# Graph attention layer, one core: where the three products of a slot group are added up

## The chip, the cores and the metric

The kernel runs on one core of a Trainium2 chip. The metric is the time of one execution on the device in microseconds (us), the median of several runs. The engines of a core run side by side, each through its own queue, and meet at semaphores: TensorE (PE in the profile, its weight loads PEld), VectorE (DVE), ScalarE (ACT), GpSimd (POOL) and SyncE (SP). All matrices here are float32.

## The reference

One layer of attention over a graph with 4096 nodes of 512 features and 8 heads of 64, a feed-forward part, and a last normalization. The mask is sparse: a node has on average some 17 neighbours (itself among them), at most about 40.

```python
hs = layer_norm(x, ln1_scale, ln1_bias)          # sources
ht = layer_norm(h_target, ln1_scale, ln1_bias)   # targets
q = (ht @ Wq + bq).reshape(T, H, HD) / jnp.sqrt(jnp.float32(HD))
k = (hs @ Wk + bk).reshape(S, H, HD)
v = (hs @ Wv + bv).reshape(S, H, HD)
logits = jnp.einsum('thd,shd->hts', q, k)
logits = jnp.where(edge_mask[None] != 0, logits, NEG)
probs = jax.nn.softmax(logits, axis=-1)
ctx = jnp.einsum('hts,shd->thd', probs, v).reshape(T, D)
ht = layer_norm(ht + ctx @ Wo + bo, ln2_scale, ln2_bias)
x = _layernorm(x + ht + jax.nn.gelu(ht @ W1) @ W2)
```

## The kernel before

**Two stages.** The first (up to about 310 us) reads the adjacency matrix, makes for every node a list of its neighbours, sorts the nodes by their number of neighbours into 32 tiles of 128 rows, and projects all sources to k and v, which go to a table in DRAM (`kvd`, 1024 numbers a row: k, then v). The second does attention and feed-forward tile by tile. The tiles are in two parts of 16: tiles 0 to 15 hold the rows of the first half of the nodes, tiles 16 to 31 (`i >= NA`) those of the second. While the first part's attention runs, the lists of the second part are still being made; from tile 16 on there is attention and feed-forward only.

**Slot groups.** A tile whose rows have up to `cap` neighbours has `cap` slots: in slot j each of the 128 rows has its j-th neighbour. The slots are taken in groups of three (`S = 3`), with one or two left over at the end of a tile. There are 211 groups, 105 of them in tiles 16 to 31, and 95 of those have three slots. GpSimd gathers a slot's rows of `kvd` with an indirect DMA (line 966) into a ring buffer, `ring`, named `kv` in the profile: 20 slots in the second part, requested five groups ahead. For each group:

- VectorE multiplies q with k (line 1218) and sums it over each head's 64 elements to the logits `lg` (line 1223).
- ScalarE takes the exponential to `p` (lines 1227 and 1236).
- In a group of three, ScalarE also makes the product of the third slot (number 2) with its own exponentials: one small exponential (line 1199) and eight multiplications, one for each head (line 1202).
- VectorE multiplies the other slots' v with p in one instruction (line 1182).
- In tiles 16 to 31 VectorE adds the product of slot 1 to that of slot 0 (line 1186).
- TensorE transposes what is left, four blocks of 128 columns for each slot, and adds them up in PSUM as it does so (`cps`, line 1190). Tiles 0 to 15 send all three slots there, tiles 16 to 31 two: slots 0 and 2.

The products of a group are made by `values`, which runs one group later than its logits: the loop in `attention` issues the logits of group k, then the products of group k-1, then asks for new gathers (`request`). `by_scalar` is issued with the logits of its own group. A tile's last group is followed by `finish`: the sums of p (lines 1080 to 1087), the context times one over the sum (line 1101), the output projection (line 1113), and the second normalization (lines 697, 680, 692 and 1131, with a power on GpSimd in line 687). `front` makes q for a tile some groups ahead (lines 966, 1000, 1009, 1014).

**Feed-forward.** `feed` takes two tiles at a time: the hidden layer (line 1323), Gelu on ScalarE (line 1326), and the output (line 1332). `_weave` merges attention and feed-forward into one program by costs written in the code; these costs are not touched by the change. A scheduler of the language then sets the order of each engine's queue by its own estimates, so that an added instruction also moves others. Each queue runs in the order so set. After the last tile's attention TensorE still has feed-forward for about two tile groups to do.

Of the kernel before, what the change touches and what calls it, by code (L numbers as in the profile page):

```python
# [443 lines left out]
def adj_resnorm_kernel(  # L444
# [33 lines left out]
    nc = tc.nc  # L478
    N, D = x.shape
# [23 lines left out]
    S = 3  # L503
# [29 lines left out]
    with tc.tile_pool(name="keep", bufs=1) as keep:  # L533
# [17 lines left out]
        with ExitStack() as late:  # L551
# [481 lines left out]
            def step(gens, i):  # L1033

                if i in gens and next(gens[i], StopIteration) is StopIteration:
                    del gens[i]

            def request(k):


                ahead = AHEAD + (1 if k >= first_b else 0)
                while issued[0] <= min(k + ahead, len(SG) - 1):
                    issue(issued[0])
                    mine = set(range(place[issued[0]], place[issued[0]] + SG[issued[0]][2]))
                    for m in range(k, issued[0]):
                        assert not mine & set(range(place[m], place[m] + SG[m][2]))
                    issued[0] += 1
# [100 lines left out]
            def go_on():  # L1148
                for i in list(fronts):
                    step(fronts, i)  # L1150
# [14 lines left out]
            def attention():  # L1165


                tails, pend = [], []

                def advance():  # L1170
                    go_on()
                    for t in list(tails):
                        if next(t, StopIteration) is StopIteration:
                            tails.remove(t)

                def values(i, j0, n, kv, p, cps, after):

                    m = n - 1 if n == S else n  # L1180
                    v4 = kv[:, :m, D:].rearrange("p j (h d) -> p j h d", h=H)
                    nc.vector.tensor_tensor(v4, v4, p[:, j0:j0 + m, :].unsqueeze(3)  # L1182
                                            .to_broadcast([P, m, H, HD]), ALU.mult)
                    slots = list(range(n))
                    if m > 1 and i >= NA:
                        nc.vector.tensor_add(kv[:, 0, D:], kv[:, 0, D:], kv[:, 1, D:])
                        slots.remove(1)
                    for j in slots:
                        for c in range(KC):
                            nc.tensor.matmul(cps[:, c, :], kv[:, j, D + c * P:D + (c + 1) * P], ident,  # L1190
                                             is_transpose=True, start=j0 + j == 0 and c == 0,
                                             stop=j0 + n == TILES[i][1] and j == slots[-1],
                                             skip_group_check=True)
                    if after is not None:
                        tails.append(after)

                def by_scalar(kv, lg):
                    pa = sp.tile([P, H], F32, name="pa")
                    nc.scalar.activation(pa, lg[:, S - 1, :], AF.Exp)
                    for hd in range(H):  # L1200
                        v = kv[:, S - 1, D + hd * HD:D + (hd + 1) * HD]
                        newest[:] = [nc.scalar.mul(v, v, pa[:, hd:hd + 1]).ins]  # L1202

                request(0)
                yield 0.0
                k = 0
                for group in GROUPS:
                    hs = []
                    mv = sp.tile([P, 2, 2], F32, name="mv2")
                    cost = 0.5 * UNIT * len(group) / 2 / sum(TILES[i][1] for i in group)  # L1210
                    for i in group:
                        cps = ps.tile([P, KC, P], F32, name="cps", bufs=2)
                        while k < len(SG) and SG[k][0] == i:
                            _, j0, n = SG[k]
                            while i not in tqs:
                                step(fronts, i)
                            kv, tq = kvs.pop(k), tqs[i]
                            nc.vector.tensor_tensor(kv[:, :n, :D], kv[:, :n, :D],  # L1218
                                                    tq[:, :D].unsqueeze(1).to_broadcast([P, n, D]),
                                                    ALU.mult)  # L1220
                            lg = sp.tile([P, S, H], F32, name="lg")
                            latest[:] = [lg[:, 0, 0:1]]
                            nc.vector.tensor_reduce(lg[:, :n, :],  # L1223
                                                    kv[:, :n, :D].rearrange("p j (h d) -> p j h d", h=H),
                                                    AX.X, ALU.add)
                            if j0 > 0:
                                nc.scalar.activation(p[:, j0:j0 + n, :], lg[:, :n, :], AF.Exp)  # L1227
                            advance()
                            yield cost * n
                            if pend:  # L1230
                                values(*pend.pop())
                                request(k)
                            advance()
                            if j0 == 0:
                                p = sp.tile([P, MAXE, H], F32, name="p", bufs=1)
                                nc.scalar.activation(p[:, :n, :], lg[:, :n, :], AF.Exp)
                            if n == S:
                                by_scalar(kv, lg)
                            last = j0 + n == TILES[i][1]
                            after = finish(i, p, cps, group, hs, mv) if last else None  # L1240
                            pend.append((i, j0, n, kv, p, cps, after))
                            yield cost * n
                            k += 1
                values(*pend.pop())
                while tails:
                    advance()
                    yield 3.0
                verdict()

            def verdict():  # L1250

                sf = sums.rearrange("p t h -> p (t h)")
                both = sp.tile([P, MAXE, H], F32, name="p", bufs=1).rearrange("p j h -> p (j h)")
                ok, over = both[:, :NT * H], both[:, NT * H:NT * H + NT]
                nc.vector.tensor_scalar(ok, sf, SUM_LO, None, op0=ALU.is_gt)
                nc.vector.scalar_tensor_tensor(ok, sf, SUM_HI, ok, op0=ALU.is_lt, op1=ALU.mult)
                nc.vector.tensor_reduce(bad[:, 3:4], ok, AX.X, ALU.min)
                nc.vector.tensor_scalar(bad[:, 3:4], bad[:, 3:4], 1.0, None, op0=ALU.not_equal)
                for i, (_, cap) in enumerate(TILES):
                    nc.vector.tensor_scalar(over[:, i:i + 1], tags[:, i, DEG:DEG + 1], float(cap),  # L1260
                                            None, op0=ALU.is_gt)
                nc.vector.tensor_reduce(bad[:, 4:5], over, AX.X, ALU.max)
                nc.vector.tensor_scalar(over, tags[:, :, DEG], 1.0, None, op0=ALU.is_lt)
                nc.vector.tensor_reduce(bad[:, 5:6], over, AX.X, ALU.max)
                b1 = sp.tile([P, 1], BF16, name="b1", bufs=1)
                nc.vector.tensor_reduce(b1, bad, AX.X, ALU.max)
                pb = ps.tile([1, 1], F32, name="t", bufs=2)
                nc.tensor.matmul(pb, b1, ones_bf[:, 0:1], start=True, stop=True)
                nc.vector.tensor_scalar(raised, pb, 0.5, None, op0=ALU.is_gt)
# [215 lines left out]
```

## Time and profile before

| | us |
|---|---|
| median of 3 runs (lowest, highest) | 1821.51 (1818.98, 1823.71) |
| the profiled execution | 1820.38 |
| its span | 1818.6 |
| TensorE busy in the span | 1686.6 (93%) |
| VectorE busy | 1435.0 (79%) |
| ScalarE busy | 1221.5 (67%) |
| GpSimd busy | 976.5 (54%) |
| first, last addition of line 1186 (start) | 1028.0, 1682.8 |

The page cuts the span into 40 equal slices of 45.5 us and gives an engine's busy share of each in tenths (9 is 90% or more); PEclk is the clock that TensorE was granted. The groups of instructions give line, engine, operation, tiles and shape, then the count, and after the bar the busy time in us and the mean of one instruction in ns; after the second bar stands the time for which the engine idled before such an instruction, and what released it. A line of the waits gives who waited for whom, the total in us, the number of waits, and the longest. Busy times of neighbours can overlap, so the distance between two starts is what one more instruction costs a full queue.

### The profile page before, as it was taken

The numbers are of one execution on the slowest core, as the hardware profiler recorded it, in microseconds if no ns is written. First come the engines' busy times: TensorE is split into PE (matmuls) and PEld (weight loads), VectorE is DVE, ScalarE is ACT, GpSimd is POOL, SyncE is SP. The second block draws the span as 40 slices with busy tenths as digits, with TensorE's granted clock in tenths as the row PEclk, the third lists the DMA queues.
The fourth block names the chain that finished last, engine by engine and source line by source line (L and its number), as shares of the span: only waits on it lengthen the run. The fifth ranks groups of instructions, "written<-read, shape, count | busy, mean of one in ns | idle before, by whom it ended". The sixth has DMA issues, their size and how long they took to land. (4 is left out here: it accounts for less than half of the span.)

```text
span 1818.6 us, 22965 instructions
## 1 busy us (share of the span) xinstructions
PE 1686.6 (93%) x7030; PEld 1100.9 (61%) x7030; DVE 1435.0 (79%) x2660; ACT 1221.5 (67%) x3119; POOL 976.5 (54%) x834
## 2 busy tenths in 40 slices
PE   7999975588999999999999989999999999999997
PEld 3444432466766666676776657666666666666664
DVE  6989866899999837787978989979879697988200
ACT  5867644486998645767878878877877576787311
POOL 1000143666465576676668788877575655764101
PEclk9999987598999999999999999999999999999999
DMA  9999958989887747677879878887786767774000
GB/s 345 366 389 370 346 171 304 405 284 324 292 303 234 238 141 269 227 267 263 289 259 316 296 258 277 261 291 266 241 268 206 262 222 242 247 248 152 18 6 26
DMA packets 140268, 463.26 MB, mean 255 GB/s; under 512 B 16500, under 2 KB 21672, under 8 KB 140136
## 3 DMA queue, kind: packets, MB, share of 16 engines
q0 software_dynamic: 96656, 342.64, 55.7%
q1 hardware_dynamic: 35664, 95.98, 15.0%
q10 hardware_dynamic: 7816, 23.08, 3.3%
q8 instruction: 58, 0.95, 0.2%
q14 instruction: 74, 0.61, 0.1%
HBM read 430.75 MB, written 30.89 MB: 254 GB/s over the span
## 5 line engine op out<-in xcount | busy, mean ns | idle before, releaser
L966 POOL DMA_INDIRECT kv<-kvd,rec x603 | 757.4, 1256 | 370.7 <-PE cps L1190 134.1
L1332 PE MATMUL po<-w,gt 128*128 128x512 f32 x1024 | 466.3, 598 | 6.6 <-ACT gt L1326 6.3
L1323 PE MATMUL pf<-h2T,w 128*128 128x256 f32 (+1 forms) x2176 | 466.5, 368 | 2.0 <-issue 1.7
L1323 PEld LDWEIGHTS pf<-h2T,w 128*128 128x128 f32 x2176 | 389.5, 191 | 66.9 <-issue 22.1
L1202 ACT ACTIVATE kv<-kv,pa 128x64 f32<-128x64 f32 x1520 | 391.0, 336 | 4.4
L1218 DVE TENSOR_TENSOR kv<-kv,tq 128x1536 f32<-128x1536 f32 (+2 forms) x211 | 352.0, 1678 | 51.0 <-DMA kv<-kvd,rec 48.4
L1223 DVE TENSOR_REDUCE lg<-kv 128x24 f32<-128x1536 f32 (+2 forms) x211 | 350.6, 1669 | 1.0
L1332 PEld LDWEIGHTS po<-w,gt 128*128 128x128 f32 x1024 | 188.9, 192 | 203.2 <-issue 195.2
L1190 PE MATMUL cps<-ident,kv 128*128 128x128 f32 x2008 | 267.5, 281 | 45.3 <-issue 22.7
L1190 PEld LDWEIGHTS cps<-ident,kv 128*128 128x128 f32 x2008 | 240.9, 146 | 112.7 <-issue 69.8
L1182 DVE TENSOR_TENSOR kv<-kv,p 128x1024 f32<-128x1024 f32 (+1 forms) x211 | 251.4, 1196 | 26.3 <-ACT p L1227 21.1
L687 POOL TENSOR_TENSOR n_rs<-n_ve,mhalf 128x2 f32<-128x2 f32 (+2 forms) x51 | 50.1, 983 | 329.8 <-DVE n_ve L680 154.5
L728 ACT ACTIVATE kv<-kv 128x1024 uint8<-128x1024 int32 x128 | 134.9, 1055 | 97.4 <-DMA kv<-in_adj_dram 49.3
L1326 ACT ACTIVATE gt<-pf 128x512 f32<-128x512 f32 x128 | 76.4, 597 | 97.1 <-PE pf L1323 74.9
L929 PE MATMUL pq<-wk,h2T 128*128 128x512 f32 x256 | 125.3, 634 | 12.3 <-ACT h2T L914 5.5
L735 DVE MAX8 cand<-kv 128x8 uint16<-128x103 uint16 (+1 forms) x640 | 133.6, 259 | 0.5
L1326 ACT ACT_TABLE_LOAD x103 | 132.1, 1283 | 1.7
L1009 PE MATMUL t<-wq,tq 128*128 128x512 f32 x256 | 117.4, 602 | 5.0 <-ACT tq L1003 4.3
L929 PE MATMUL pq<-wv,h2T 128*128 128x512 f32 x256 | 115.3, 593 | 0.6 <-ACT tq L931 0.6
L1113 PE MATMUL t<-wo,rb 128*128 128x512 f32 x256 | 115.2, 592 | 0.0
L1227 ACT ACTIVATE p<-lg 128x24 f32<-128x24 f32 (+2 forms) x179 | 39.1, 219 | 105.7 <-DVE lg L1223 83.3
L929 PEld LDWEIGHTS pq<-wk,h2T 128*128 128x128 f32 x256 | 50.4, 204 | 78.1 <-issue 59.0
(159 smaller groups left out, 1582.2 us busy)
## 6 DMA issues: line engine op xcount, KB each, us to landing
kv<-in_adj_dram SPq DMA_DIRECT2D x128, 512.0 KB
kvd<-tq ACTq DMA_DIRECT2D x24, 512.0 KB
kv<-kvd,rec POOLq DMA_INDIRECT x603
kv<-in_L_gnn_h_target_dram SPq DMA_DIRECT2D x32, 256.0 KB
kv<-in_x_dram SPq DMA_DIRECT2D x15, 512.0 KB
rest_d<-gid SPq DMA_DIRECT2D x32, 160.0 KB
w<-in_L_gnn_W_dram SPq DMA_DIRECT2D x4, 1024.0 KB
kvd<-kv ACTq DMA_DIRECT2D x8, 512.0 KB
```

The lines of the kernel that those rows point to most:

```text
L728: nc.scalar.activation(sg, a, AF.Sign, accum_out=dpart[:, i, h:h + 1])
L735: nc.vector.max(cand[:, h * SQ + s, :], wd[:, w0:w1])
L929: nc.tensor.matmul(pkv, hT[:, kc, j * P:(j + 1) * P], w[:, kc, :], start=kc == 0, stop=kc == KC - 1)
L966: nc.gpsimd.indirect_dma_start(out=dst, out_offset=None, in_=table[:, :], in_offset=bass.IndirectOffsetOnAxis(ap=idx, axis=0))
L1182: nc.vector.tensor_tensor(v4, v4, p[:, j0:j0 + m, :].unsqueeze(3) .to_broadcast([P, m, H, HD]), ALU.mult)
L1190: nc.tensor.matmul(cps[:, c, :], kv[:, j, D + c * P:D + (c + 1) * P], ident, is_transpose=True, start=j0 + j == 0 and c == 0, stop=j0 + n ...
L1202: newest[:] = [nc.scalar.mul(v, v, pa[:, hd:hd + 1]).ins]
L1218: nc.vector.tensor_tensor(kv[:, :n, :D], kv[:, :n, :D], tq[:, :D].unsqueeze(1).to_broadcast([P, n, D]), ALU.mult)
L1223: nc.vector.tensor_reduce(lg[:, :n, :], kv[:, :n, :D].rearrange("p j (h d) -> p j h d", h=H), AX.X, ALU.add)
L1323: nc.tensor.matmul(pf[:, k, :], w1[(f0 + k) // KC][:, kc, (f0 + k) % KC * P:((f0 + k) % KC + 1) * P], h2T[:, kc, :w], start=kc == 0, stop= ...
L1326: nc.scalar.activation(gt, pf, AF.Gelu_apprx_tanh)
L1332: nc.tensor.matmul(po[j], gt[:, k, j * P:(j + 1) * P], w2[(f0 + k) // KC][:, (f0 + k) % KC, :], start=False, stop=f0 + k == FC - 1, skip_g ...
```

## The change

In a group of three slots in tiles 16 to 31, VectorE adds the product of slot 2 to slot 0 as well, with a second addition after the one of line 1186. TensorE then transposes slot 0 alone: four transposes instead of eight. Groups of one or two slots, and all groups of tiles 0 to 15, are as before. Lines after the addition move down by three; the second addition is line 1189 of the changed kernel.

```diff
                     if m > 1 and i >= NA:
                         nc.vector.tensor_add(kv[:, 0, D:], kv[:, 0, D:], kv[:, 1, D:])
                         slots.remove(1)
+                        if n == S:
+                            nc.vector.tensor_add(kv[:, 0, D:], kv[:, 0, D:], kv[:, S - 1, D:])
+                            slots.remove(S - 1)
                     for j in slots:
                         for c in range(KC):
                             nc.tensor.matmul(cps[:, c, :], kv[:, j, D + c * P:D + (c + 1) * P], ident,
```

## The prediction

> **What bounds the kernel now.** I read the page's slices first, then the second part cut into stretches, then its groups, then who waits for whom, then single instructions. All times are those of the one profiled execution: span 1818.6 us, 1820.38 us with what lies around it, 1.1 us under the median of three runs (1821.51 us).
>
> The slices, the page's second section:
>
> ```profile
> PE   7999975588999999999999989999999999999997
> DVE  6989866899999837787978989979879697988200
> PEclk9999987598999999999999999999999999999999
> ```
>
> The additions of line 1186 run only from 1028 to 1683 us, so only slices 23 to 37 can change. TensorE is full there, VectorE nearly; the last two and a half slices are TensorE alone. The same in numbers: busy time by stretch (columns: stretch, its length, then busy time and instructions of TensorE, of its weight loads, of VectorE, ScalarE and GpSimd, then granted clock, DMA share, GB/s):
>
> ```profile
> 1028.00:1178.00 150.00, 142.06 (x621) 96.67 (x620) 143.55 (x148) 122.39 (x335) 124.57 (x88) 0.98 0.83 274
> 1178.00:1328.00 150.00, 145.81 (x621) 97.68 (x620) 129.95 (x150) 115.15 (x306) 104.19 (x89) 0.99 0.77 254
> 1328.00:1478.00 150.00, 146.87 (x630) 99.70 (x629) 121.42 (x139) 105.66 (x281) 94.50 (x82) 0.99 0.75 250
> 1478.00:1628.00 150.00, 150.00 (x639) 100.92 (x638) 125.09 (x138) 109.06 (x293) 92.37 (x79) 1.00 0.72 239
> 1628.00:1700.00 72.00, 71.83 (x312) 48.82 (x311) 53.61 (x100) 48.21 (x124) 25.83 (x21) 1.00 0.40 132
> 1700.00:1818.60 118.60, 105.49 (x446) 70.27 (x444) 7.18 (x26) 20.73 (x40) 10.58 (x12) 0.96 0.06 19
> ```
>
> From 1028 to 1700 us TensorE is busy 656.6 of 672 us and VectorE 573.6. The reader is to see that the balance moves: in the first stretch VectorE is the fuller one (143.6 against 142.1), later TensorE. So TensorE bounds most of this part, VectorE its first fifth, and the margin between them is small everywhere.
>
> The groups the change touches, from 1028 to 1700 us:
>
> ```profile
> L1190 PE MATMUL cps<-ident,kv 128*128 128x128 f32 x789 | 104.4, 275 | 6.7 <-DVE kv L1186 6.6
> L1182 DVE TENSOR_TENSOR kv<-kv,p 128x1024 f32<-128x1024 f32 x100 | 121.6, 1220 | 14.1 <-ACT p L1227 14.1
> L1186 DVE TENSOR_TENSOR kv<-kv 128x512 f32<-128x512 f32 x101 | 68.8, 684 | 0.2
> ```
>
> **What the Trainium skill says.** "VectorE: DVE Perf Modes", section on the TRN2 errata, gives an fp32 tensor_tensor add as (N+151)/0.96 ns, 691 ns for 512 elements; the 684 ns above agree. "TensorE: Matmul & The Clock Gate", its table at the head, calls the queues of ScalarE and VectorE strict FIFOs: an instruction that waits holds all behind it. The order on both engines in the trace fits that. "SBUF — State Buffer", Who interferes with whom, says that a VectorE instruction with two SBUF inputs contends with a GpSimd instruction that reads SBUF; the new additions are of that kind. The gathers of line 966 take 933 ns at the least and 1285 ns in the mean here, but GpSimd is busy 441 of 672 us, so I give this no time.
>
> **The change part by part.** Tiles 16 to 31 have 95 groups of three slots. The order of the built program has 380 transposes fewer on TensorE and 95 additions more on VectorE, and nothing more or less on the other engines.
>
> TensorE, removed: single instructions (start, duration) give the price, since the 275 ns of one overlap the next.
>
> ```profile
> 1211.17 1.04 PE L1190 MATMUL cps<-ident,kv 128*128 128x128 f32 x8
> ...
> 1241.81 0.60 PE L1190 MATMUL cps<-ident,kv 128*128 128x128 f32 x4
> ```
>
> Four transposes more cost 1.04 - 0.60 = 0.44 us, so 95 groups save 41.8 us of TensorE's queue, not the 104 us that 380 times 275 ns would give. That comes to 6% of its work between 1028 and 1700 us. The tail is not touched: after the last transpose of line 1190 the built program has the same matmuls as before, and the tail's 118.6 us stay.
>
> VectorE, added: two neighbours of the same size start 0.60 us apart, though each lasts 0.68.
>
> ```profile
> 1139.44 0.68 DVE L1186 TENSOR_TENSOR kv<-kv 128x512 f32<-128x512 f32 x1
> 1140.04 0.68 DVE L1223 TENSOR_REDUCE lg<-kv 128x8 f32<-128x512 f32 x1
> ```
>
> I take 0.61 us, so 58 us for 95; VectorE goes from 573.6 to 631.6 us, TensorE from 656.6 to 614.8. The bound changes hands.
>
> The new wait: the second addition needs slot 2, which ScalarE multiplies head by head (line 1202, eight instructions); before, only TensorE read that row. Start, duration, engine:
>
> ```profile
> 1203.70 0.57 ACT L1202 ACTIVATE kv<-kv,pa 128x64 f32<-128x64 f32 x2
> 1204.29 1.28 ACT L1326 ACT_TABLE_LOAD   x1
> ...
> 1206.07 1.92 ACT L1144 ACTIVATE h2T<-t,cols 128x256 f32<-128x256 f32 x4
> ...
> 1206.39 0.68 DVE L1186 TENSOR_TENSOR kv<-kv 128x512 f32<-128x512 f32 x1
> ...
> 1207.87 1.55 ACT L1202 ACTIVATE kv<-kv,pa 128x64 f32<-128x64 f32 x6
> ```
>
> Here two products were done, then a table load, a Gelu and four copies came between, and the last product ended at 1209.42, 2.35 us after the first addition. Taken over the 95 groups, the products end after their first addition in 26, by 37.7 us together; by more than 1.7 us (one q times k product, which the new order usually puts between the two additions) in 8, by 10.4 us beyond it. So the wait costs between 0 and 38 us; I take 10 us for VectorE. Behind the waiting addition stand the next logits' reduction (line 1223) and the next product with p (line 1182); ScalarE's exponentials wait for the one, TensorE's transposes for both.
>
> The buffer's slot 2 now comes free with the second addition, slot 0 still with TensorE's transposes, which wait longer. The gathers are issued 11 us or more (19.5 in the median) before VectorE reads them, so a few microseconds are covered by that lead. If the cover went, the waits of line 1218 on its gathers, now 10.2 us, would grow; I count 0, at most 10.
>
> Order: the scheduler also pulls feed-forward matmuls forward. Before the transposes of slot group 123 (of 211) the program has some 28 more of them, counted in units of about 0.44 us (a pair of the 256-wide ones; sixteen last 3.62 us in the trace), and it is level again from group 179. That moves some 12 us of TensorE's work into the stretch where VectorE is the bound, and is worth about 4 us later.
>
> The sum, by stretch, with 24.5, 21.6, 19.8, 19.8 and 9.4 groups (the counts of line 1186, 26, 23, 21, 21 and 10, times 95/101): VectorE gets 158.5, 143.1, 133.5, 137.2, 59.3; TensorE 131.3, 136.3, 138.2, 141.3, 67.7. The larger ones make 648.8 us, if nothing idles. In the first stretch VectorE, the fuller engine, idled 4.3%. I charge that where VectorE leads or is within 5 us, 5% in the third, 2% in the last: 165.6 + 149.5 + 145.5 + 147.7 + 69 = 677.3, against 672: +5.3. Less 4 for the order, plus 10 for the wait, is +11: 1820.4 + 11 = 1831 us.
>
> **Rivals.**
> - TensorE stays the bound (faster). VectorE idled 98 us in these 672, and 30 of them were for a late TensorE: the waits on line 1009 and, through ScalarE, on line 1113.
>
> ```profile
> DVE kv L1182 <- ACT p L1227: 17.7, 11, 3.6
> DVE tq L1014 <- PE t L1009: 17.3, 5, 6.2
> DVE n_nm L692 <- POOL n_rs L687: 13.9, 7, 4.3
> DVE n_st L697 <- ACT h L1118: 12.6, 3, 6.1
> ```
>
> If the 58 us fit into that slack, the first stretch costs about 162 (2% idle), the others 146, 141, 141 and 68: 658, so -14, 1806 us. For it: 1278 to 1328 us, where VectorE was busy 47.6 of 50 us while TensorE never stopped. Against it: the remaining waits (ScalarE's p, GpSimd's powers) don't come from TensorE and stay.
> - Even: the idle share of the first stretch holds everywhere and the new wait falls into time VectorE would idle anyway: 1821 us.
> - The in-order wait spreads (slower, far). VectorE waits for products that stand on ScalarE behind a Gelu, which waits for TensorE, which waits in order for transposes behind the same addition. It decides from where the wait reaches its upper bound of 38 us and the old 68 us of other idle time stay: 631.6 + 38 + 68 = 738, +66; half of that wait and 50 us of the idle time give 701, +29: 1849 us.
> - That the change doesn't do what it says is excluded by the built order.
>
> **How the numbers follow.** VectorE as bound, +4 to +24 us: 0.45. Spread wait, +24 to +50: 0.15. Even: 0.18. TensorE's gain shows: 0.22, down to 1804. A measurement of this kernel tells 0.3%, 5.5 us, from no change. Part of the first case lies within it (0.03): slower 0.57, same 0.21, faster 0.22. Range 1804 to 1856; the likeliest case alone is 1824 to 1844.
>
> **What would show it.** Right: line 1190 has 1628 transposes, the new addition 95 times at 0.68 us; VectorE at 93% or more between 1028 us and the last addition; TensorE with waits of tens of microseconds on line 1189; waits of line 1189 on line 1202 near 10 us; the tail unchanged. Wrong: TensorE still at 98% there (then the time falls), or VectorE under 90% with long waits on line 1202 (then it rises more).

## The result, and the profile after

The changed kernel takes 1838.76 us (median of 11 runs, 1827.11 to 1843.23) against 1823.21 us before (11 runs, 1818.98 to 1830.21): ratio 1.0076, 95% interval 1.0054 to 1.0097 (the two medians alone give 1.0085). It is slower, by some 15.5 us where 9.5 were forecast. The two profiled executions lie a little further apart than the medians: the span is 1839.4 us, 20.8 more than before.

The slices of the changed kernel's page (as before, tenths of 40 equal slices):

```profile
PE   7999884598999998999999989979999899989997
DVE  6999867899998848777879989979989798988400
PEclk9999987698999999999999999989998999999998
```

Busy time by stretch of the changed kernel, with the columns of the prediction's table; the part that can change now ends at 1718 instead of 1700 us:

```profile
1028.00:1178.00 150.00, 137.51 (x550) 88.90 (x548) 141.69 (x161) 115.01 (x313) 110.99 (x82) 0.98 0.79 257
1178.00:1328.00 150.00, 135.43 (x520) 86.99 (x520) 135.73 (x158) 112.37 (x293) 118.18 (x85) 0.93 0.77 250
1328.00:1478.00 150.00, 132.92 (x516) 86.91 (x515) 131.33 (x155) 108.14 (x281) 113.73 (x83) 0.93 0.75 246
1478.00:1628.00 150.00, 142.76 (x559) 92.83 (x558) 140.30 (x174) 117.64 (x310) 106.77 (x75) 0.98 0.71 231
1628.00:1718.00 90.00, 82.98 (x315) 52.92 (x314) 77.62 (x125) 63.68 (x160) 40.91 (x33) 0.96 0.53 174
1718.00:1839.40 121.40, 108.36 (x457) 72.70 (x455) 7.90 (x30) 22.58 (x42) 11.30 (x13) 0.96 0.06 19
```

TensorE is no longer full, and VectorE is not full either: in every stretch both idle, by 7 to 19 us of 150, and almost equally. Two engines that idle together point to a common wait. From 1028 to 1718 us VectorE is busy 626.7 of 690 us, before 573.6 of 672: 53 us more work, 35 us less idle time, and the part is 18 us longer. The other 3 us of the span lie within the last row.

Where the idle time is, the waits of the changed kernel from 1028 to 1725 us say (who for whom: total us, times, longest):

```profile
ACT h L1131 <- DVE n_nm L692: 62.6, 8, 12.0
DVE n_nm L692 <- POOL n_rs L687: 53.5, 8, 10.2
...
PEld cps L1193 <- DVE kv L1189: 36.5, 24, 9.5
...
PE cps L1193 <- DVE kv L1189: 25.1, 7, 9.1
...
PE t L1140 <- ACT h L1131: 23.2, 7, 10.4
```

53.5 of VectorE's 63 us of idle time are one kind of wait: the mean of the second normalization (line 692) waits for GpSimd's power (line 687). Before, VectorE idled 21.7 us at line 692; the profile finds no releaser ("issue") for one of these waits, of 7.8 us:

```profile
L692 DVE SCALAR_TENSOR_TENSOR n_nm<-mv,n_rs 128x2 f32<-128x2 f32 x8 | 1.3, 160 | 21.7 <-POOL n_rs L687 13.9 <-issue 7.8
```

All its other waits together shrank from 77 to 10 us.

The second addition, in the groups of instructions over the same time, doesn't wait (0.1 us idle before it):

```profile
L1189 DVE TENSOR_TENSOR kv<-kv 128x512 f32<-128x512 f32 x95 | 65.0, 685 | 0.1
```

One of the eight waits in order of time, from the timeline of the changed kernel (start, duration, engine, instruction, and in brackets the idle time before it and its releaser):

```profile
1198.62 3.17 PE L1335 MATMUL po<-w,gt 128*128 128x512 f32 x7
...
1200.67 0.69 DVE L1186 TENSOR_TENSOR kv<-kv 128x512 f32<-128x512 f32 x1
...
1201.89 0.94 POOL L966 DMA_INDIRECT kv<-kvd,rec  x1 [0.30 <-PE po L1335]
1203.14 0.94 POOL L966 DMA_INDIRECT kv<-kvd,rec  x1 [0.31 <-issue]
1204.38 0.94 POOL L966 DMA_INDIRECT kv<-kvd,rec  x1 [0.30 <-issue]
1205.63 0.94 POOL L966 DMA_INDIRECT kv<-kvd,rec  x1 [0.30 <-issue]
1206.87 0.94 POOL L966 DMA_INDIRECT kv<-kvd,rec  x1 [0.30 <-issue]
1208.11 0.94 POOL L966 DMA_INDIRECT kv<-kvd,rec  x1 [0.30 <-issue]
1209.36 0.94 POOL L966 DMA_INDIRECT kv<-kvd,rec  x1 [0.30 <-issue]
1210.31 0.74 POOL L687 TENSOR_TENSOR n_rs<-n_ve,mhalf 128x2 f32<-128x2 f32 x1
1211.09 0.16 DVE L692 SCALAR_TENSOR_TENSOR n_nm<-mv,n_rs 128x2 f32<-128x2 f32 x1 [9.72 <-POOL n_rs L687]
...
1211.28 1.52 ACT L1131 ACTIVATE h<-h,n_nm,n_rs 128x512 f32<-128x512 f32 x2 [10.92 <-DVE n_nm L692]
...
1212.15 0.47 PE L1140 MATMUL t<-ident,h 128*128 128x128 f32 x1 [10.37 <-ACT h L1131]
```

The reader is to see that for some nine microseconds none of the compute engines works but GpSimd, which issues seven gathers, one every 1.24 us, before it comes to a power of two columns. The power's input had been ready since 1196.4. VectorE, ScalarE and TensorE each stand, in their own order, at the instruction that needs it.

In the built order the power's place is hardly new: before and after, it stands on GpSimd's queue behind the gathers that lie about five slot groups ahead of VectorE, and line 692 on VectorE zero to four instructions behind the variance. What is new is that GpSimd is behind when the power is asked for. Before, in four of the eight tile groups after 1028 us GpSimd began the power 0.15 us after its input was ready, with no DMA issued in between; now it does so in one, and in the other seven it first issues three to ten DMAs, and the power begins 3.7 to 13.9 us after its input. VectorE is in step with those places, where before it was often late for other reasons, TensorE among them. And GpSimd has become slower: a gather of line 966 takes 1395 ns in the mean where it took 1285.

### The profile page after: what moved, and what is told of

Same layout as the page of the kernel before. It is cut to its first block, busy times and chain, and to the rows that moved or that the text cites. A ratio compares the mean times of both kernels' runs of the same rounds, so it can differ in the third digit from the quotient of the medians.

```text
span 1839.4 us, 22352 instructions
## 1 busy us (share of the span) xinstructions
PE 1660.0 (90%) x6650; PEld 1062.8 (58%) x6650; DVE 1486.0 (81%) x2755; ACT 1237.1 (67%) x3129; POOL 1029.2 (56%) x834
## 5 line engine op out<-in xcount | busy, mean ns | idle before, releaser
L966 POOL DMA_INDIRECT kv<-kvd,rec x603 | 793.2, 1315 | 355.2 <-issue 119.9
L1335 PE MATMUL po<-w,gt 128*128 128x512 f32 x1024 | 479.9, 608 | 10.9 <-ACT gt L1329 10.9
L1326 PE MATMUL pf<-h2T,w 128*128 128x256 f32 (+1 forms) x2176 | 474.0, 370 | 0.3 <-ACT h2T L1144 0.3
L1193 PE MATMUL cps<-ident,kv 128*128 128x128 f32 x1628 | 225.9, 283 | 65.7 <-DVE kv L1182 40.3
L1193 PEld LDWEIGHTS cps<-ident,kv 128*128 128x128 f32 x1628 | 198.1, 146 | 134.6 <-DVE kv L1182 44.6
L687 POOL TENSOR_TENSOR n_rs<-n_ve,mhalf 128x2 f32<-128x2 f32 (+2 forms) x51 | 46.2, 905 | 319.2 <-DVE n_ve L680 151.1
```

The lines of the kernel that those rows point to most:

```text
L966: nc.gpsimd.indirect_dma_start(out=dst, out_offset=None, in_=table[:, :], in_offset=bass.IndirectOffsetOnAxis(ap=idx, axis=0))
L1326: nc.tensor.matmul(pf[:, k, :], w1[(f0 + k) // KC][:, kc, (f0 + k) % KC * P:((f0 + k) % KC + 1) * P], h2T[:, kc, :w], start=kc == 0, stop= ...
L1335: nc.tensor.matmul(po[j], gt[:, k, j * P:(j + 1) * P], w2[(f0 + k) // KC][:, (f0 + k) % KC, :], start=False, stop=f0 + k == FC - 1, skip_g ...
```

## The experiments

Three theories at the outset. *Queue*: the change loses because VectorE, now full, stands in order for a power that is stuck on GpSimd behind gathers. *Work*: VectorE's 58 us of additions set the time, and the standing only fills time that it would idle anyway. *Order*: any edit makes the scheduler lay the queues anew, and the luck of that order is what is measured. All ratios are to the kernel before, with 95% intervals.

**Line 692 later, in the changed kernel.**

```diff
                 rs = power(sp, mv[:, :nh, :], nh, "n2", ve)
                 yield
+                yield
+                yield
+                yield
+                yield
                 nm = negmean(sp, mv[:, :nh, :], rs, nh, "n2")
```

> The changed kernel, with the mean of the second normalization (line 692) and what follows it emitted four half-groups later after GpSimd's power (line 687); nothing else differs. Theory, queue: the changed kernel loses because VectorE, now full, stands at line 692 for a power that waits on GpSimd behind gathers (53.5 us in eight waits). Then these waits fall below 10 us, the last addition moves forward by 35 to 45 us, and the time is 1795 to 1810 us, ratio to before 0.985 to 0.993. Rival, work: VectorE's 58 us of additions set the time and the standing only fills time that it would idle anyway: 1830 to 1840 us, ratio 1.004 to 1.009.

Measured: 1802.23 us, ratio 0.9884 (0.9857 to 0.9910), within what *queue* gives. The waits of VectorE from 1028 to 1730 us:

```profile
DVE n_st L697 <- ACT h L1118: 18.7, 1, 18.7
DVE n_nm L692 <- POOL n_rs L687: 11.0, 3, 9.6
```

and the second stretch, busy time by engine as above:

```profile
1178.00:1328.00 150.00, 148.50 (x589) 93.47 (x588) 150.00 (x180) 126.36 (x327) 123.02 (x92) 1.00 0.80 275
```

The standing falls from 53.5 to 11 us, not quite below 10, and VectorE is busy for 150 of 150 us, TensorE for 148.5. *Work* is refuted: the same additions are done in less time than before the change. The last transposes of context end at 1673.3 us instead of 1722.3; the stretch after them has grown from 117.1 to 127.3 us. This version computes all that the reference asks for and beats both kernels. But its queues are laid anew in large part, so that this run alone doesn't part *queue* from *order*.

**The same half way: two half-groups later.**

> The changed kernel with line 692 and what follows emitted two half-groups later in place of four; seven to nine instructions of VectorE then stand between the variance and line 692, against two to four in the changed kernel and thirteen in the later version. Theory, queue: a dose in between: standing of 10 to 30 us, 1808 to 1825 us, ratio 0.991 to 1.000. Rival, order: the later version's 0.9884 was luck of the new order, and this one does not lie between them.

Measured: 1815.25 us, 0.9948 (0.9934 to 0.9963); VectorE stands 24.7 us at line 692. With 53.5, 24.7 and 11.0 us of standing the three versions take 1838.8, 1815.3 and 1802.2 us: a dose and its effect, into which luck of the order would hardly fall.

**The same edit in the kernel before.**

> The kernel before, with the same later place of line 692. Theory, queue: TensorE bounds this kernel, so the 21.7 us for which VectorE stands there between 1028 and 1700 us are worth little: 1810 to 1823 us, ratio 0.993 to 1.000. If later normalizations starve the feed-forward part: up to 1835 us. Rival, work: no change, 0.998 to 1.002.

Measured: 1853.65 us, 1.0162 (1.0135 to 1.0189); a miss. The edit didn't do here what it was for: the scheduler put line 692 directly behind the variance all the same in four of the first seven tile groups, and the standing grew to 35.2 us. The stretch after the last transposes grew by 10 us here as well (127.1 against 117.3 us). What else costs the time was not pursued. So an edit that lays the queues anew can cost over one per cent, and the later version's gain can't be taken to be the wait's alone; the next runs had to touch the wait with less disturbance.

**The product of line 692 on GpSimd**, in the changed kernel and in the kernel before:

```diff
+                ng = sp.tile([P, nh], F32, name="n2_ng")
+                nc.vector.tensor_scalar_mul(ng, mv[:, :nh, 0], -1.0)
                 yield
                 rs = power(sp, mv[:, :nh, :], nh, "n2", ve)
+                nm = sp.tile([P, nh], F32, name="n2_nm")
+                nc.gpsimd.tensor_tensor(nm, ng, rs, ALU.mult)
                 yield
-                nm = negmean(sp, mv[:, :nh, :], rs, nh, "n2")
```

> The changed kernel with the product of line 692 (minus mean times power) made by GpSimd right behind its power; VectorE makes only minus the mean, beforehand. VectorE no longer waits for GpSimd's power, but ScalarE still does at line 1131, in its own queue, and TensorE at line 1140. Theory, queue: the 53.5 us of standing at line 692 are gone; about half comes back as waits of VectorE for ScalarE's exponentials that stand behind line 1131: 1808 to 1825 us, ratio to before 0.991 to 1.001. If VectorE's own place in the queue was all: 1790 to 1805 us. Rival, work: no change against the changed kernel, 1834 to 1842 us.

> The kernel before with the same product on GpSimd. Theory, queue: with TensorE as bound the standing of VectorE is worth at most some us: 1812 to 1825 us, ratio 0.994 to 1.001. Rival, order: any such edit makes the scheduler lay the queues anew, and that alone moves the time by a per cent either way, as the later place of line 692 did in the kernel before (1.0162): then this lies outside 0.994 to 1.001.

Measured: changed 1865.24 us, 1.0216 (1.0196 to 1.0237); before 1832.04 us, 1.0037 (1.0020 to 1.0053). Both miss the expectation of *queue*; the second lies just outside its range, as *order* had it. The waits of the first show where the time went, ScalarE's and then VectorE's (in this version's numbers 1131 is the new product on GpSimd, 1134 the scaling on ScalarE that was line 1131, 1208 ScalarE's product of slot 2, 1192 the second addition, 1185 the product with p, 1242 the exponential of a tile's first group):

```profile
ACT h L1134 <- POOL n_nm L1131: 88.0, 7, 16.7
```

```profile
DVE kv L1192 <- ACT kv L1208: 29.0, 5, 11.5
DVE kv L1185 <- ACT p L1242: 26.4, 5, 8.0
```

Taken off VectorE, the wait passes to ScalarE, the next in line, and lasts longer: 88 us in seven waits, where ScalarE stood 62.6 us at this scaling in the changed kernel. VectorE then stands for what is queued on ScalarE behind it, its second addition too. In the kernel before, ScalarE stands 24.5 us for the new product. So it isn't enough to take the wait off VectorE: whichever engine reads the power's result soon after it is asked for waits for GpSimd's queue. Why the wait became longer, and what the two added instructions cost, was not separated.

**No power at all**, in both kernels; nothing is added anywhere:

```diff
-                rs = power(sp, mv[:, :nh, :], nh, "n2", ve)
+                rs = ve
                 yield
```

> The changed kernel without GpSimd's power in the second normalization: the variance stands in for its power minus one half, so that the power is left out of the arithmetic and nothing of this step lies on GpSimd's queue; no instruction is added anywhere. Theory, queue: the standing at line 692 (53.5 us), ScalarE's at line 1131 and TensorE's at line 1140 go, whoever is next: 1785 to 1803 us, ratio to before 0.979 to 0.989. Rival, VectorE's work sets the time: over 1815 us.

> The kernel before without GpSimd's power in the second normalization, edited in the same way. Theory, queue: the standing there was 21.7 us of VectorE's time, mostly in the shadow of a busy TensorE: 1808 to 1822 us, ratio 0.991 to 0.999. Then the change, freed of the power, is faster than before freed of it by 10 to 25 us. If before gains as much as the changed kernel does (35 us and more), the power isn't what turned the change's sign.

Measured: changed 1803.04 us, 0.9876 (0.9858 to 0.9894); before 1818.17 us, 0.9969 (0.9958 to 0.9980). The first two stretches of the changed kernel without the power:

```profile
1028.00:1178.00 150.00, 143.46 (x572) 92.93 (x571) 149.93 (x169) 121.33 (x329) 121.17 (x84) 0.99 0.79 261
1178.00:1328.00 150.00, 143.89 (x569) 92.69 (x568) 146.37 (x173) 120.02 (x316) 118.74 (x91) 0.99 0.83 281
```

This decides the case. Line 692 now follows the variance with no idle time of note before it, in both kernels. Without the power the changed kernel gains 35.7 us (1838.76 to 1803.04), the kernel before 6.6 us (1824.75 in the runs beside it to 1818.17). Freed of it, the change is faster than its own base by 15 us (1803.04 against 1818.17, 0.9876/0.9969 = 0.991); with it, slower by 15.5. The wait for the power turned the sign. The order of the queues is an unlikely cause, for it hardly changes: from 1028 us on, GpSimd's 349 other instructions stand in the traces of the changed kernel with and without the power in the same order, and only some 25 of VectorE's 797 and 200 of TensorE's 2900 stand elsewhere; in the pair of the kernel before it is 2, 21 and 11. Nor is it GpSimd's slower gathers by themselves: without the power they take 1393 ns in the mean, as slow as with it. The changed kernel's median lies at the upper edge of what was expected, since other waits take up part of it: 12.0 us for line 1118, 11.5 for line 1098, 15.0 for gathers.

**The two halves of the change.** The addition alone goes into slot 1, which nobody reads any more; the removal alone leaves out slot 2's product:

```diff
-                            nc.vector.tensor_add(kv[:, 0, D:], kv[:, 0, D:], kv[:, S - 1, D:])
-                            slots.remove(S - 1)
+                            nc.vector.tensor_add(kv[:, 1, D:], kv[:, 1, D:], kv[:, S - 1, D:])
```

```diff
-                            nc.vector.tensor_add(kv[:, 0, D:], kv[:, 0, D:], kv[:, S - 1, D:])
                             slots.remove(S - 1)
```

> The second addition alone: slot 2 is added into slot 1, which nobody reads any more, and TensorE transposes slots 0 and 2 as before. 95 additions more on VectorE, no transpose less. If the 42 us saved on TensorE are worth something in the changed kernel, this one is slower than it: 1845 to 1870 us, ratio 1.012 to 1.026. If VectorE and its standing alone set the changed kernel's time, it is equal to it: 1835 to 1842 us, ratio 1.006 to 1.010. The longer use of slot 2 by TensorE can cost a little in the gathers.

> The removal alone: groups of three in tiles 16 to 31 leave out slot 2's product, there is no second addition and TensorE transposes slot 0 alone. 380 transposes less, 42 us of TensorE's queue. If TensorE bounds the part from 1028 us on: 1780 to 1795 us, ratio 0.977 to 0.985. If VectorE's standing for GpSimd's power takes its place at once: 1800 to 1812 us, ratio 0.988 to 0.994.

Measured: addition alone 1844.05 us, 1.0112 (1.0089 to 1.0134); removal alone 1803.64 us, 0.9882 (0.9859 to 0.9905). The addition costs 1.1%, the removal gains 1.2%, as the second of its two expectations has it. Each makes the standing at line 692 grow by itself, from 21.7 us to 39.2 with the addition and to 38.0 with the removal. The sum would be nil; together they cost 0.76%. The addition's result lies between its two expectations, so how much of TensorE's saving is left in the changed kernel is not settled: 0 to 0.8% by the intervals.

**No wait for ScalarE's products.** The second addition reads slot 1 again instead of slot 2:

```diff
-                            nc.vector.tensor_add(kv[:, 0, D:], kv[:, 0, D:], kv[:, S - 1, D:])
+                            nc.vector.tensor_add(kv[:, 0, D:], kv[:, 0, D:], kv[:, 1, D:])
```

> The changed kernel, but the second addition reads slot 1 again in place of slot 2: as many additions and transposes, and no wait of VectorE for ScalarE's products; slot 2's product is left out. The prediction put that wait at 10 us; the trace of the changed kernel shows no idle time before line 1189. If the prediction's term is right: 6 to 12 us faster than the changed kernel, 1827 to 1833 us. If the trace is: equal within 4 us, 1835 to 1843 us, ratio 1.005 to 1.011.

Measured: 1836.45 us (22 runs, 1820.71 to 1844.83), 1.0051 (1.0036 to 1.0067). Its interval overlaps the changed kernel's, as the trace of that kernel had it. The difference of the medians is 2.3 us, and VectorE still stands 48.5 us at line 692. The new wait that the prediction feared most is worth a few microseconds at most.

**Later, except in the last tiles.** As the first experiment, with `if i < NT - 3:` around the four half-groups, to win back the 10 us by which the closing stretch had grown:

> The changed kernel with line 692 four half-groups later, except in the last two tile groups, whose normalization stands ahead of the closing feed-forward part. The later version's stretch after its last transpose of context was 127 us against 117 in the changed kernel. If the four half-groups in the last tiles make those 10 us: 1790 to 1797 us, ratio 0.981 to 0.986. If not: equal to the later version, 0.986 to 0.991.

Measured: 1812.65 us (13 runs, 1803.87 to 1822.02), 0.9934 (0.9916 to 0.9952); a miss. The stretch after the last transposes is still 127 us long, so the place in the last tiles doesn't make it; and the standing at line 692 is 19.9 us instead of 11.0, though the built order of GpSimd's queue is the same and that of the others nearly so. Why is open; the two versions were measured on different chips. But with the order nearly unchanged the time goes with the standing again: 11.0, 19.9 and 24.7 us of it in the three later versions, 1802, 1813 and 1815 us.

## Why the prediction was right, and where not

*What bounds before*: held. With the power away the change is faster, which only the removal of the transposes can make, since the addition is work that comes on top.

*The prices*: held for VectorE. The 95 additions take 685 ns each, VectorE's busy time rises by 53 us where 58 were counted, and the closing stretch after the last transposes is as long as before (117.1 us against 117.3). TensorE's busy time in the part that can change falls from 656.6 to 631.6 us, by 25 us where 42 were counted, since the feed-forward matmuls of lines 1326 and 1335 take 18 us more there (464 against 446 us), at a lower granted clock. The prediction had no term for that.

*The new wait, 10 us*: wrong, the term that failed first. The trace shows 0.1 us before line 1189, and the run without the wait can't be told from the changed kernel. The estimate took the products' lag from the old trace, where they end after their first addition in 26 of 95 groups. In the changed kernel they do in nine, by 9 us together, and nearly all of that lies within the product of q and k (1.7 us) between the two additions. Why the lag became shorter was not separated.

*VectorE's idle time, 4.3% taken over from the first stretch*: mis-sized, and of another kind. Measured 63 of 690 us, 9.2%, of which 53.5 us are the wait for the power. Its row stood among the waits that the prediction showed (13.9 us; 21.7 us of idle time at line 692 in all), and the prediction said that such waits "stay". It grew to two and a half times the 21.7 us instead. The step that failed is that a wait on an in-order queue was carried over as a constant: here it grew as the waiting engine came into step with the queue that it waits for.

*GpSimd "I give this no time"*: wrong in size. 285 gathers at 110 ns more are 31 us of GpSimd's queue, the very queue on which the power waits. By themselves they cost little, as the run without the power shows. How much of the standing comes from this and how much from VectorE's being in step was not separated.

*The gathers' lead*: held for VectorE, whose waits on gathers went from 10.2 to 3.1 us (the lead was under 11 us in two of 103 groups, at the least 6.9, which changes nothing). But the same five groups of lead are the backlog in front of the power.

*The signs*: TensorE's waits of tens of microseconds on line 1189, the counts and the tail came as said. VectorE at 93% or more did not: it was busy for 90.8% up to the last addition. Neither did the waits of line 1189 on ScalarE.

*The sum*: +11 against +15.5 in the medians, and +20.8 between the two traces: right in sign and roughly in size, for half of the right reasons. That it came out so is in part luck. Its 683 us for the part that can change hold 52 us of VectorE's idle time, where 63 were measured, but 10 of them are a wait that wasn't there, and most of the measured ones are a wait that was to stay as it was. Without the 10 us the same sum would have said +1, no change. The rival of the spreading in-order wait had the right mechanism with the wrong partner: GpSimd's queue, not ScalarE's. The rival in which TensorE's gain shows gave 1806 us; the later version and the one without the power reach 1802 and 1803.

## What to carry to other kernels

When work moves to an engine that was slack, ask which in-order waits its slack was hiding: a tiny operation on a queue full of DMA issues costs little while its reader is late (6.6 us here) and much once the reader is in step (35.7 us). Before giving up such a change, give that operation distance from its reader, or take it off that queue; here distance turned +0.8% into -1.2%, and so did leaving the operation out. But such an edit lays the queues anew, and in the kernel before the same one cost 1.6%: look at where the scheduler has put the reader. Moving only the reader to the next engine passes the wait on.

## What the runs showed of the hardware

How long a gather's issue on GpSimd takes goes with what VectorE does. Between 1028 and 1660 us of the changed kernel the 74 gathers of line 966 whose first 0.94 us no two-operand product or addition of VectorE (TENSOR_TENSOR) overlapped took 0.94 to 1.00 us; the 203 others took 1.57 us in the mean, at most 4.95. The power itself can be held up in the same way. In the later version's timeline:

```profile
1198.29 0.68 DVE L1190 TENSOR_TENSOR kv<-kv 128x512 f32<-128x512 f32 x1
1198.60 3.22 POOL L687 TENSOR_TENSOR n_rs<-n_ve,mhalf 128x2 f32<-128x2 f32 x1
1198.88 1.75 DVE L1225 TENSOR_TENSOR kv<-kv,tq 128x1536 f32<-128x1536 f32 x1
...
1200.55 0.68 DVE L1193 TENSOR_TENSOR kv<-kv 128x512 f32<-128x512 f32 x1
...
1201.15 1.74 DVE L1230 TENSOR_REDUCE lg<-kv 128x24 f32<-128x1536 f32 x1
```

It takes 3.22 us under a row of such instructions and ends 0.67 us after the reduction, which has one operand, has begun; another in this run, at 1642.69 us, took 3.83 and ended in the same way. In the wait shown further up, with VectorE standing, it took 0.74. And TensorE's granted clock was 0.93 in the two stretches of the changed kernel in which it stood most (1178 to 1478 us), against 0.99 before, and the feed-forward product of 512 columns took 608 ns in the mean of the whole run, before 598. The other versions go the same way: from 1178 to 1328 us the clock was 0.87 with TensorE busy for 117.3 of 150 us (product of line 692 on GpSimd) and 1.00 with 148.5 (line 692 later). So in these runs a TensorE that stands now and then also works more slowly.
